# Eigenvalue counts beside a dense matmul stream: first loads on two queues, longer stated times, last products in twos, the last three groups in steps

**Chip and metric.** One core of a Trainium2 chip (trn2). The metric is the device time of one execution, in microseconds (us); lower is better. All numbers are medians of runs in the fast state unless a single profiled execution is named.

## The reference

Four residual layers, each `x = layernorm(x + layer(x))`, on x of 128 x 64 x 256 in fp32, with one 64 x 64 adjacency for all.

```python
# layer 0: three graph convolutions with adj*adj, widths 256 -> 512 -> 1024 -> 256
# layer 1: spectral: eigenvectors U of the normalised Laplacian, U (relu(U^T x W1 + b1) W2 + b2)
_, U = jnp.linalg.eigh(L_norm)
agg = jnp.einsum('mn,bnd->bmd', U.T, features)
# layer 2: two graph convolutions, then LSTMs over windows of 1, 2, 3 and 4 nodes
# layer 3: masked attention over the 64 nodes with shared h = x W + b
attention = jax.nn.softmax(scores, axis=2)
return jnp.einsum('bnm,bmd->bnd', attention, h) + b
```

## The kernel before

The rows of x are 64 tiles of 128 x 256. The kernel runs in two stages. In the first, layer 0 goes through 32 groups of two tiles, two groups in flight, and beside it runs the eigenvalue stream: the 64 x 64 matrix is made tridiagonal, the eigenvalues are bracketed by six passes of counting signs (a chain of small VectorE instructions and no matmul at all), then a recurrence gives the eigenvectors. In the second stage 16 groups of four tiles go through layers 1 to 3, three in flight.

TensorE's order is fixed while the program is built. Each stream is a generator; it yields the stated time at which its next matmul may come. A virtual clock `now` advances with each matmul:

```python
def mm(out, lhsT, rhs, start=True, stop=True):
    PE.matmul(out, lhsT, rhs, start=start, stop=stop)
    now[0] += 2 * max(0.0009 * rhs.free_size(), 0.112)
...
with tc.manual_schedule(engines={mybir.EngineType.PE}):      # TensorE, and no other engine
    while todo or going or eig:
        ...
        streams = ([eig] if eig else []) + going
        able = [x for x in streams if x[0] <= now[0] + 0.05]
        pick = able[0]          # or the earliest, and now moves on to it
```

The argument turns on the `with` line: the fixed order holds for TensorE only. Where the instructions of the other engines stand in their queues is decided by the framework.

The counts (`after(n)` adds 0.21 us per instruction to the stream's stated time):

```python
for k in range(1, N):
    V.reciprocal(r, Q[:, k - 1, :])
    V.scalar_tensor_tensor(Q[:, k, :], r, es[:, 0, k:k + 1], Q[:, k, :], op0=ALU.mult, op1=ALU.add)
    if k % 2:
        yield after(5)
```

The end of a layer 0 group; L626 is the addition, and the pool `psa` has five PSUM tiles:

```python
        S.copy(s3, p)
        yield now[0] + 1.5
        p = tl(psa, [P, 2, D], "ps")
        mm(p, sqT2, s3)
        V.tensor_add(xs, p, xs)                 # L626
        rows_norm(tc, small, xs, half)
```

The end of layer 3 (L911) and the choice among the last three groups:

```python
            for j in range(2):
                mm(p[:, j, :], eT[:, (t + j) * P:(t + j + 1) * P], hn[:, t + j, :])
                V.scalar_tensor_tensor(xs[:, t + j, :], p[:, j, :], sm[...], xs[:, t + j, :], ...)   # L911
...
    pick = able[0] if todo else min(able, key=lambda x: x[1])     # x[1]: turns taken so far
```

Of the kernel before, what the change touches and what calls it, by code (L numbers as in the profile page):

```python
# [39 lines left out]
def eigen(tc, stack, a, cst, u2, ut2, now):  # L40
# [8 lines left out]
    nc = tc.nc  # L49
# [10 lines left out]
    def ps(shape, tag):  # L60
        uid[0] += 1
        return pp.tile(shape, F32, tag=tag, name=f"{tag}_{uid[0]}")
# [6 lines left out]
    def after(n, turns=0):  # L69

        clock[0] += 0.21 * n + 0.6 * turns
        return clock[0] + 0.3
# [8 lines left out]
        V.scalar_tensor_tensor(junk, x, 1.0, y, op0=ALU.mult, op1=ALU.mult, accum_out=out)  # L81


    aT = ps([N, N], "pa")
    PE.transpose(aT, a, C["eye"])
    s2 = sb([N, N], "s2")
# [47 lines left out]
    for i in range(N - 2):  # L134
        j = i + 1
# [135 lines left out]
    for _ in range(PASSES):  # L271
        V.tensor_scalar(h, h, 1.0 / (FAN + 1), None, op0=ALU.mult)
        x = sb([N, FAN], "bx")
        V.tensor_scalar(x, C["idx"][:, 1:FAN + 1], h, lo, op0=ALU.mult, op1=ALU.add)
        V.tensor_tensor(Q, di[:, 0, :].unsqueeze(2).to_broadcast([N, N, FAN]),
                        x.unsqueeze(1).to_broadcast([N, N, FAN]), ALU.subtract)
        for k in range(1, N):
            r = sb([N, FAN], "br")
            V.reciprocal(r, Q[:, k - 1, :])  # L279
            V.scalar_tensor_tensor(Q[:, k, :], r, es[:, 0, k:k + 1], Q[:, k, :], op0=ALU.mult, op1=ALU.add)  # L280
            if k % 2:
                yield after(5)
        V.scalar_tensor_tensor(M.rearrange("p j k -> p k j"), Q, 0.0, inb.unsqueeze(2).to_broadcast([N, N, FAN]),
                               op0=ALU.is_lt, op1=ALU.mult)
        cnt = sb([N, FAN], "bx")
        V.tensor_reduce(cnt, M, AX.X, ALU.add)
        V.scalar_tensor_tensor(sb([N, FAN], "br"), cnt, tgt, C["ones"][:, :FAN], op0=ALU.is_le, op1=ALU.mult,
                               accum_out=co_[6])
        V.tensor_scalar(lo, co_[6], h, lo, op0=ALU.mult, op1=ALU.add)
        yield after(20)  # L290
# [8 lines left out]
    for k in range(1, N):  # L299
        c = N - 1 - k  # L300
        t = sb([N, 2], "tw")
        V.reciprocal(t, D[:, :, c + 1])
        V.tensor_mul(t, t, es[:, :, k])  # L303
        V.tensor_add(D[:, :, c], dl[:, :, k], t)
        if k % 2:
            yield after(6)
    V.tensor_scalar(D, D, 1e15, -1e15, op0=ALU.min, op1=ALU.max)
    V.tensor_add(t0, D[:, 0, ::-1], D[:, 1, :])
    V.tensor_sub(t0, t0, dl[:, 0, :])
# [20 lines left out]
    V.tensor_sub(zh, zd, oh)  # L330
    V.tensor_add(zh, zh, zu[:, ::-1])
    rowdot(nrm, zh, zh)
    yield after(24)
    pz = ps([N, N], "pa")
    PE.transpose(pz, zh, C["eye"])
    Z = cp.tile([N, N], F32, name="Z")
# [42 lines left out]
    rowdot(s1, zh, v1)  # L379
    rowdot(s1s, zh, v1s)  # L380
    rowdot(s2e, zh, v2)
    after(34)


    V.reciprocal(co_[6], nrm)
# [25 lines left out]
    V.tensor_mul(co_[12], co_[12], rn)  # L411


    yield after(16)
    pu = ps([N, N], "pa")
    mm(pu, Z, QT)
    UT = cp.tile([N, N], F32, name="UT")
    V.tensor_scalar(UT, pu, co_[12], None, op0=ALU.mult)
    yield after(1)
    pt = ps([N, N], "pb")  # L420
    PE.transpose(pt, UT, C["eye"])
    U = cp.tile([N, N], F32, name="U")
    V.tensor_copy(U, pt)
    V.memset(u2, 0.0)
    V.memset(ut2, 0.0)
    yield after(4, 1)
    for out, lhsT in ((u2, UT), (ut2, U)):
        p2 = ps([2 * N, N], "pa")
        for h in range(2):
# [7 lines left out]
D = 256  # L437
EPS = 1e-5
WAYS = 3


def rows_norm(tc, pool, x, half):
# [17 lines left out]
def kernel(  # L460
# [25 lines left out]
    nc = tc.nc  # L486
    V, S, PE = nc.vector, nc.scalar, nc.tensor
    NT = ROWS // P
    x_t = x.rearrange("b n f -> (b n) f").rearrange("(t p) f -> p t f", p=P)
# [22 lines left out]
    X = keep.tile([P, NT, D], F32, name="X")  # L512
# [2 lines left out]
    adst = keep.tile([P, N], F32, name="adst")  # L515
    a64 = ea.tile([N, N], F32, name="a64")
    eig_c = ea.tile([P, len(CONSTS), N], F32, name="eig_c")
    nc.sync.dma_start(a64, adj)
    for h in range(2):
        hs = slice(h * N, (h + 1) * N)  # L520
        nc.sync.dma_start(ad2[hs, hs], adj)
    nc.sync.dma_start(X[:, 0:2, :], x_t[:, 0:2, :])
    aw1 = load(wa, "aw1", a_w1, "(k p) f -> p k f", [P, 2, 512], p=P)
    nc.sync.dma_start(eig_c, consts)
    aw2 = wa.tile([P, 4, 1024], F32, name="aw2")
    for h in range(2):
        cols = slice(h * 512, (h + 1) * 512)
# [47 lines left out]
# [3 lines that stand above are left out]
# [53 lines left out]
    todo = [layer0(g) for g in range(NT // 2)]  # L631
    eig = [0.0, eigen(tc, phase_a, a64, eig_c, u2, ut2, now)]
    going = []
    with tc.manual_schedule(engines={mybir.EngineType.PE}):
        while todo or going or eig:
# [3 lines left out]
            able = [x for x in streams if x[0] <= now[0] + 0.05]  # L639
            if able:  # L640
                pick = able[0]
            else:
                pick = min(streams, key=lambda x: x[0])
# [32 lines left out]


    now[0] = 0.0
    MOVE, MIXED, LIN, CONV, NORM, SOFT = 1.2, 1.2, 1.5, 1.8, 4.5, 4.5
    CELL = {256: 2.6, 168: 2.2, 128: 1.9}  # L680

    def turn(out, in_):
# [12 lines left out]
    def as3(t, a):  # L695
        return t.rearrange("p (a b) -> p a b", a=a)
# [153 lines left out]
    def layer3(xs, g, ready):  # L850
        xT = as3(work(), 2)
        ps = [ps4() for _ in range(2)]
        for t in range(4):
            if t % 2 == 0:
                yield ready[t // 2]
            for k in range(2):
                turn(ps[k][:, t * P:(t + 1) * P], xs[:, t, k * P:(k + 1) * P])
        V.tensor_copy(xT[:, 0, :], ps[0])
        S.copy(xT[:, 1, :], ps[1])
        nc.gpsimd.tensor_tensor(xs, xs, wide["d_b"].unsqueeze(1).to_broadcast([P, 4, D]), ALU.add)  # L860
        yield now[0] + MOVE
        hT = as3(work(), 2)
        for c in range(2):
            p = ps4()
            run(p, [(dw[:, k, c * P:(c + 1) * P], xT[:, k, :]) for k in range(2)])
            S.activation(hT[:, c, :], p, AF.Identity, bias=dbl[:, c, :])
            yield now[0]
        yield now[0] + MOVE
        p = ps4((P, 4, N))
        for t in range(4):  # L870
            for h in range(2):
                cols = slice(t * P + h * N, t * P + (h + 1) * N)
                for k in range(2):
                    PE.matmul(p[h * N:(h + 1) * N, t, :], hT[:, k, cols], hT[:, k, cols], start=k == 0, stop=k == 1)  # L874
        now[0] += 1.5
        sc = as3(work2(), 8)
        s, z = sc[:, 0:4, :], sc[:, 4:8, :]
        V.tensor_mul(s, p, adst.unsqueeze(1).to_broadcast([P, 4, N]))
        V.tensor_scalar(z, s, 0.0, -1e16, op0=ALU.is_equal, op1=ALU.mult)
        V.tensor_add(s, s, z)  # L880
        mx = small.tile([P, 4], F32, name="mx")
        V.tensor_reduce(mx, s, AX.X, ALU.max)
        V.tensor_sub(s, s, mx.unsqueeze(2).to_broadcast([P, 4, N]))
        e = att[g % WAYS]
        for h in range(2):
            hs = slice(h * N, (h + 1) * N)
            S.activation(e[hs, :, hs], s[hs, :, :], AF.Exp)  # L887
        yield now[0]
        ready = now[0] + SOFT
        hn = as3(work(), 4)  # L890
        for t in range(0, 4, 2):
            p = ps4((P, 2, D))
            for j in range(2):
                for c in range(2):
                    turn(p[:, j, c * P:(c + 1) * P], hT[:, c, (t + j) * P:(t + j + 1) * P])
            S.copy(hn[:, t:t + 2, :], p)
        yield ready
        sm = small.tile([P, 4], F32, name="sm")
        p = ps4()
        for t in range(4):  # L900
            turn(p[:, t * P:(t + 1) * P], e[:, t, :])
        eT = work2()
        S.copy(eT, p)
        V.tensor_reduce(sm, e, AX.X, ALU.add)
        V.reciprocal(sm, sm)
        yield now[0] + MOVE
        for t in range(0, 4, 2):
            p = ps4((P, 2, D))
            for j in range(2):
                mm(p[:, j, :], eT[:, (t + j) * P:(t + j + 1) * P], hn[:, t + j, :])  # L910
                V.scalar_tensor_tensor(xs[:, t + j, :], p[:, j, :], sm[:, t + j:t + j + 1], xs[:, t + j, :],  # L911
                                       op0=ALU.mult, op1=ALU.add)
            rows_norm(tc, small, xs[:, t:t + 2, :], half)
            nc.sync.dma_start(out_t[:, 4 * g + t:4 * g + t + 2, :], xs[:, t:t + 2, :])
            yield now[0]

    def group(g):
        xs = X[:, 4 * g:4 * g + 4, :]
        ready = yield from layer1(xs)
        ready = yield from layer2(xs, ready)  # L920
        yield from layer3(xs, g, ready)



    todo = [group(g) for g in range(NT // 4)]
    going = []
    with tc.manual_schedule(engines={mybir.EngineType.PE}):
        while todo or going:
            while todo and len(going) < WAYS:
                going.append([0.0, 0, todo.pop(0)])  # L930
            able = [x for x in going if x[0] <= now[0] + 0.05]
            if not able:
                pick = min(going, key=lambda x: x[0])
                now[0] = pick[0]
            else:
                pick = able[0] if todo else min(able, key=lambda x: x[1])
            try:
                pick[0] = next(pick[2])
                pick[1] += 1
            except StopIteration:  # L940
                going.remove(pick)
# [42 lines left out]
```

## Time and profile before

| | before |
|---|---|
| time, median of the first three runs | 2721.07 us |
| TensorE busy in the profiled execution (2721.1 us) | 2593.5 us |
| TensorE idle, 0 to 68 us (start) | 14.8 us |
| TensorE idle, 408 to 748 us (counts to eigenvectors) | 31 us |
| TensorE idle, last slice of 68 us | 29 us |

The shares, slices and waits are shown in the prediction. There each digit of a slice row is a busy share in tenths, and PEclk is TensorE's granted clock, the share of full speed that it was allowed to run at (so 0.50 is half clock). The word *turn* is used twice: for the step that a stream gets from the scheduler, and for a transposition on TensorE (the function `turn`), as in "the norm's turn". A *cell* is an LSTM step. Two places of the timeline are worth a look of their own. Its columns are start, length, engine, line, operation, names, shapes, number of instructions and, in brackets, the engine's idle time before the row and what ended it. First TensorE in the count phase:

```profile
442.41 1.02 PE L576 MATMUL ps<-s,sqT 128*128 128x512 f32 x2
443.27 1.05 PE L576 MATMUL ps<-sqT,X 128*128 128x128 f32 x8
444.16 1.06 PE L576 MATMUL ps<-sqT,h 128*128 128x128 f32 x8
449.35 1.01 PE L576 MATMUL ps<-sqT,h 128*128 128x128 f32 x3 [4.13 <-DVE X L626]
```

And VectorE's (DVE) addition in the same stretch:

```profile
448.62 0.68 DVE L626 TENSOR_TENSOR X<-ps,X 128x512 f32<-128x512 f32 x1
```

The last product of a group (`ps<-s,sqT`) is done at 443.4, VectorE reads it at 448.62, 5.2 us later. In between TensorE has used the other four PSUM tiles, and it stands for 4.13 us until the fifth has been read. Then the end of layer 3 in the steady second stage:

```profile
1556.81 0.59 PE L576 MATMUL ps<-w,v 128*128 128x256 f32 x2
1558.43 1.13 PE L576 MATMUL ps<-w,v 128*128 128x256 f32 x4 [1.03 <-DVE X L911]
1560.14 0.70 PE L576 MATMUL ps<-w,v 128*128 128x256 f32 x2 [0.58 <-DVE X L911]
```

Each product waits until VectorE has read the one before it out of the same PSUM tile: 1.03 + 0.58 us per group.

### The profile page before, as it was taken

To read this page: it belongs to the slowest core of one execution; us is meant where nothing else is said; L and a number is where in the kernel's file an instruction comes from. 1 tells how busy PE (TensorE), PEld (TensorE's weight loads), DVE (VectorE), ACT (ScalarE), POOL (GpSimd) and SP (SyncE) were. 2 spreads that over 40 slices of the span, in tenths; PEclk is the share of its full clock that TensorE was granted. 3 is DMA by queue.
4 is the path that set the end of the run, shared out by engine and by line. 5 is a ranking of instruction groups with operands and counts; after the bars stand their busy time and mean duration, and the time that the engine had idled before them with its cause. 6 is when DMAs were issued, how large, how long until landed. Compare 5 with 4: busy or idle time off the path is not lost.

```text
span 2721.1 us, 39771 instructions
## 1 busy us (share of the span) xinstructions
PE 2593.5 (95%) x15384; PEld 2256.5 (83%) x15384; DVE 1334.8 (49%) x5277; ACT 1029.7 (38%) x2525; POOL 239.8 (9%) x336
## 2 busy tenths in 40 slices
PE   7999999999899989999999999999999999999995
PEld 6888877777688878898898898898898988978993
DVE  5777768888401033444444434445444444442335
ACT  2222222222122224544444544544444444445442
POOL 0000000000000020111101101101101101110012
PEclk9999999999899999999999999999999999999996
DMA  8000000000000010000000000000000000000000
GB/s 267 1 1 1 1 1 1 1 1 1 1 1 0 1 47 1 1 9 9 9 1 8 4 6 9 1 9 9 1 9 9 1 9 9 1 9 1 1 1 24
DMA packets 24398, 32.19 MB, mean 12 GB/s; under 512 B 2336, under 2 KB 21024, under 8 KB 24208
## 3 DMA queue, kind: packets, MB, share of 16 engines
q1 hardware_dynamic: 24032, 29.19, 3.2%
q8 instruction: 121, 1.98, 0.3%
q0 software_dynamic: 176, 0.46, 0.1%
q14 instruction: 69, 0.57, 0.1%
HBM read 21.25 MB, written 8.39 MB: 11 GB/s over the span
## 4 chain that ended last, share of the span: by engine, by line
PE 48%; DVE 4%; ACT 3%; POOL 2%; issue 1%; POOLq 0%; DVEq 0%; ACTq 0%
PE ps L576 47%; PE ps L683 1%; POOL ln_rs L453 1%; DVE X L455 1%; ACT gates L782 1%; DVE X L911 1%; ACT L887 1%; ACT L782 1%; DVE X L845 1%; PE ps L874 1%; DVE ln_st L450 1%; ACT att L887 0%; POOL ln_rs L452 0%; ACT gates L790 0%; DVE ln_mv L451 0%
## 5 line engine op out<-in xcount | busy, mean ns | idle before, releaser
L576 PE MATMUL ps<-w,wih 128*128 128x128 f32 (+2 forms) x4992 | 894.1, 319 | 3.5 <-DVE w L801 3.5
L576 PEld LDWEIGHTS ps<-w,wih 128*128 128x128 f32 x4992 | 763.8, 191 | 51.6 <-issue 10.1
L782 ACT ACTIVATE gates<-ps,cbi 128x128 f32<-128x128 f32 (+2 forms) x1248 | 500.4, 410 | 549.7 <-PE ps L576 542.1
L576 PE MATMUL ps<-hs,whh 128*128 128x128 f32 (+2 forms) x3072 | 537.5, 303 | 0.0
L576 PEld LDWEIGHTS ps<-hs,whh 128*128 128x128 f32 x3072 | 454.8, 191 | 24.9 <-issue 10.5
L576 PE MATMUL ps<-m,aw 128*128 128x256 f32 x2048 | 456.4, 381 | 2.1 <-DVE tw L303 2.1
L576 PEld LDWEIGHTS ps<-m,aw 128*128 128x128 f32 x2048 | 386.2, 190 | 64.2 <-issue 11.4
L584 ACT ACTIVATE h<-ps 128x256 f32<-128x256 f32 (+1 forms) x320 | 136.5, 426 | 445.3 <-PE ps L576 445.3
L576 PE MATMUL ps<-aw,h 128*128 128x256 f32 x1024 | 228.9, 380 | 0.0
L576 PEld LDWEIGHTS ps<-aw,h 128*128 128x128 f32 x1024 | 193.2, 190 | 36.7 <-issue 12.2
L787 DVE TENSOR_TENSOR gates<-gates 128x256 f32<-128x256 f32 (+2 forms) x256 | 92.6, 362 | 221.8 <-ACT gates L782 221.4
L452 POOL TENSOR_SCALAR ln_rs<-ln_mv 128x2 f32<-128x2 f32 x128 | 29.6, 231 | 1447.6 <-DVE ln_mv L451 1245.6
L455 DVE TENSOR_SCALAR X<-X,ln_mv,ln_rs 128x256 f32<-128x256 f32 x256 | 100.9, 433 | 107.2 <-POOL ln_rs L453 107.1
L790 ACT ACTIVATE gates<-c 128x128 f32<-128x128 f32 (+2 forms) x288 | 98.1, 341 | 96.1 <-DVE c L789 84.7
L801 DVE TENSOR_TENSOR w<-gates 128x256 f32<-128x256 f32 (+2 forms) x160 | 61.7, 395 | 147.7 <-PE ps L576 109.2
L626 DVE TENSOR_TENSOR X<-ps,X 128x512 f32<-128x512 f32 x32 | 21.8, 681 | 225.7 <-PE ps L576 225.7
L576 PE MATMUL ps<-aw,m 128*128 128x512 f32 x256 | 128.7, 628 | 0.0
L786 DVE TENSOR_TENSOR c<-c,gates 128x128 f32<-128x128 f32 (+2 forms) x192 | 63.8, 332 | 129.6 <-ACT gates L782 127.3
L792 DVE TENSOR_TENSOR hs<-gates 128x128 f32<-128x128 f32 (+2 forms) x192 | 62.9, 328 | 105.0 <-ACT gates L790 74.6
L837 POOL COPY w<-w 128x512 f32<-128x512 f32 x32 | 35.6, 1119 | 816.0 <-DVE w L801 594.3
L450 DVE BATCH_NORM_STATS2 ln_st<-X 128x6 f32<-128x256 f32 x256 | 99.5, 409 | 1.3
L279 DVE RECIPROCAL br<-Q 64x16 f32<-64x16 f32 x378 | 92.3, 244 | 12.2
(324 smaller groups left out, 2658.8 us busy)
## 6 DMA issues: line engine op xcount, KB each, us to landing
X<-in_x_dram SPq DMA_DIRECT2D x32, 256.0 KB, 6.2
out_dram<-X SPq DMA_DIRECT2D x32, 256.0 KB, 2.1
wih<-in_c_ih_dram SPq DMA_DIRECT2D x4, 1024.0 KB, 8.3
aw<-in_a_w_dram SPq DMA_DIRECT2D x3, 1024.0 KB, 11.3
whh<-in_c_hh_dram SPq DMA_DIRECT2D x3, 1024.0 KB, 5.5
aw<-in_a_w_dram SPq DMA_DIRECT2D x1, 512.0 KB, 6.7
cw<-in_c_w_dram SPq DMA_DIRECT2D x2, 256.0 KB, 4.0
bw<-in_b_w_dram SPq DMA_DIRECT2D x2, 128.0 KB, 4.2
```

What stands on the lines that cost most here:

```text
L279: V.reciprocal(r, Q[:, k - 1, :])
L450: nc.vector.bn_stats(st[:, t, :], x[:, t, :])
L455: nc.vector.tensor_scalar(x[:, t, :], x[:, t, :], mv[:, t, 0:1], rs[:, t:t + 1], op0=ALU.subtract, op1=ALU.mult)
L576: PE.matmul(out, lhsT, rhs, start=start, stop=stop)
L584: S.activation(dst, src, AF.Relu)
L782: S.activation(gate[q][:, h, :], pp, AF.Tanh if q == "g" else AF.Sigmoid, bias=bias[:, j:j + 1])
L786: V.tensor_mul(c[:, h, :], c[:, h, :], gate["f"][:, h, :])
L787: V.tensor_mul(to, gate["i"][:, h, :], gate["g"][:, h, :])
L790: S.activation(gate["i"][:, h, :], c[:, h, :] if p > 1 else to, AF.Tanh)
L792: V.tensor_mul(new[:, h, :], gate["o"][:, h, :], gate["i"][:, h, :])
L801: V.tensor_mul(hT[:, h, slice(first + p - 1, first + nw * p, p), :], gate["o"][:, h, :].rearrange("p (w b) -> p w b", b=8), gate["i"][:, h ...
L837: nc.gpsimd.tensor_copy(as3(hb[:, k, :], 8), hT[:, k, :, :].rearrange("p n b -> p b n"))
```

## The change

Five parts: the small first loads go out on ScalarE's queue beside SyncE's, and the eigenvalue stream starts at 4.0; the eigenvalue stream states longer times, so that TensorE should not wait for it; NORM and SOFT, the stated times of a norm and a softmax, grow; both products of a pair in layer 3 come before both reads; of the last three groups, the older ones lead by five turns.

```diff
+    yield 4.0
     aT = ps([N, N], "pa")
 ...
-                yield after(5)          # pair of count steps
+                yield after(6)
 ...
-            yield after(6)              # pair of recurrence steps
+            yield after(9)
 ...                                     # and 24->40, 34->44, 16->24, 1->3, (4, 1)->(8, 1)
-    nc.sync.dma_start(a64, adj)
 ...                                     # ad2, as before
-    nc.sync.dma_start(X[:, 0:2, :], x_t[:, 0:2, :])
+    for t in range(2):
+        nc.scalar.dma_start(X[:, t, :], x_t[:, t, :])
 ...                                     # aw1, as before
-    nc.sync.dma_start(eig_c, consts)
+    nc.scalar.dma_start(a64, adj)
+    nc.scalar.dma_start(eig_c, consts)
 ...
-    MOVE, MIXED, LIN, CONV, NORM, SOFT = 1.2, 1.2, 1.5, 1.8, 4.5, 4.5
+    MOVE, MIXED, LIN, CONV, NORM, SOFT = 1.2, 1.2, 1.5, 1.8, 5.2, 4.8
 ...
                 mm(p[:, j, :], eT[:, (t + j) * P:(t + j + 1) * P], hn[:, t + j, :])
+            for j in range(2):
                 V.scalar_tensor_tensor(xs[:, t + j, :], p[:, j, :], sm[...], xs[:, t + j, :],
 ...
+LEAD = 5
-                going.append([0.0, 0, todo.pop(0)])
+                going.append([0.0, 0, todo.pop(0), NT // 4 - len(todo)])
-                pick = able[0] if todo else min(able, key=lambda x: x[1])
+                pick = able[0] if todo else min(able, key=lambda x: x[1] + LEAD * x[3])
```

More of the change, by code (lines that the diff above doesn't have):

```diff
@@ L332, in eigen @@
     rowdot(nrm, zh, zh)
-    yield after(24)
+    yield after(40)
     pz = ps([N, N], "pa")
@@ L381, in eigen @@
     rowdot(s2e, zh, v2)
-    after(34)
+    after(44)
     V.reciprocal(co_[6], nrm)
@@ L411, in eigen @@
     V.tensor_mul(co_[12], co_[12], rn)
-    yield after(16)
+    yield after(24)
     pu = ps([N, N], "pa")
@@ L418, in eigen @@
     V.tensor_scalar(UT, pu, co_[12], None, op0=ALU.mult)
-    yield after(1)
+    yield after(3)
     pt = ps([N, N], "pb")
@@ L425, in eigen @@
     V.memset(ut2, 0.0)
-    yield after(4, 1)
+    yield after(8, 1)
     for out, lhsT in ((u2, UT), (ut2, U)):
```

## The prediction

> **What bounds the kernel now.** I began with the page: busy shares, then the 40 slices.
>
> ```profile
> PE 2593.5 (95%) x15384; PEld 2256.5 (83%) x15384; DVE 1334.8 (49%) x5277; ACT 1029.7 (38%) x2525; POOL 239.8 (9%) x336
> PE   7999999999899989999999999999999999999995
> DVE  5777768888401033444444434445444444442335
> PEclk9999999999899999999999999999999999999996
> ```
>
> TensorE is the bound nearly everywhere. Its order is fixed at build time by a virtual clock: each stream states when its next matmul may come, and the oldest (or the eigenvalue stream, always first) that is due gets the turn. So only TensorE's idle time, 2721.1 - 2593.5 = 128 us, and time at a low clock can be won. The table by stage (68 us each) says where it lies: 14.8 us in the first slice; 4.1, 4.1, 5.7, 5.8 and 11.5 in the slices from 408 to 748, where VectorE is 87% busy with the eigenvalue counts; 7.7 at the change to layers 1 to 3; about 2.7 a slice in their steady state; 29 in the last slice. The waits of TensorE give the causes, first of the whole run and then of 1020 to 2440 us:
>
> ```profile
> PE ps L576 <- DVE X L911: 26.8, 32, 1.8
> PE ps L683 <- DVE X L455: 23.4, 17, 4.0
> PE ps L576 <- DVE X L626: 17.6, 4, 5.7
> PE pa L85 <- DMA eig_c<-in_consts_dram: 11.0, 1, 11.0
> PE pa L335 <- DVE w L331: 11.0, 1, 11.0
> ...
> PE ps L576 <- DVE X L911: 20.1, 26, 1.0
> PE ps L683 <- DVE X L455: 10.9, 11, 1.0
> ```
>
> The columns are total us, times, longest. L626 and L331 are the count phase, L911 the last products of layer 3, L455 the norms, L85 the start. The table of short windows shows the second loss, the clock (its column PEclk follows the engines):
>
> ```profile
> 449.30:454.30 5.00, 4.95 (x12) 3.22 (x13) 4.06 (x19) 0.75 (x2) 0.93 (x2) 0.50 0.00 0
> 454.30:459.30 5.00, 5.00 (x24) 4.26 (x23) 4.36 (x19) 1.36 (x3) 0.00 (x0) 1.00 0.00 0
> 2646.60:2721.10 74.50, 41.95 (x230) 25.93 (x229) 41.27 (x117) 14.73 (x27) 23.48 (x32) 0.70 0.07 22
> ```
>
> After the 4.1 us wait at 449 TensorE ran 5 us at half clock: 12 matmuls where the next window has 24. In the last 74.5 us the clock averages 0.70.
>
> **What the Trainium skill says.** "TensorE: Matmul & The Clock Gate", section What's actually happening: the array's clock is halved after an idle window of about 3.4 us and restored after a busy one. The trace agrees (the two windows above), so a long wait costs more than its length. "PSUM — Partial Sum Buffer", section PSUM bank collisions: different engines must be kept apart by bank, not by address. The two 128x256 halves of a layer 3 pair fill one 2 KiB bank, so the second product must wait for VectorE's read of the first if it comes after it; the trace has that wait 32 times. "Perfetto Trace Analysis", Optimization Strategy: a bubble that repeats can mean too few PSUM buffers; at L626 it is so, layer 0 has five and TensorE stops at the one that L626 has not yet read, four times. "DMA: Bandwidth & Descriptors", Issuing engines are not separate DMA queues: a second issuer saves issue time only. The trace before has one big issuer; its packets already move 385 to 410 GB/s from 8 us on, so I expect no more bandwidth.
>
> **The change, part by part.**
>
> 1. Counts, after(5) to after(6) and others. A pair of count steps is stated at 5 x 0.21 = 1.05 us, a pass as 32 x 1.05 + 20 x 0.21 = 37.8. Stated time is not real time: a layer 0 group states 29.5 us, but has 130 matmul instructions, and the undisturbed slices from 748 on do 318 in 68 us, so 27.8 us: a factor 0.94. VectorE thus gets 35.6 us for a pass, but its reciprocals (L279) start a new pass every 42.6 us (405.1 to 618.0 in five). It falls 7 us behind per pass, and layer 0's addition L626 in the same queue starts 5 to 7 us late at 449, 511, 574 and 636, exactly the four waits. With 6: 32 x 1.26 + 4.2 = 44.5 stated, 42.0 real against 42.6, so nearly balanced; I leave 3 us for short remaining waits. The recurrence, 32 x 9 x 0.21 = 60.5 stated, 57 real, against 38 on VectorE (658.8 to 696.7), now has room to catch up, and after(40) gives 7.9 us for a chain of 4.5: the 11.0 at L335 and 2.1 at L303 go. Half clock: about 20 us were busy at it after these waits (5 after 449, 3.4 after 512, 5.7 after 575, 5.7 after 701), half of that, some 10 us, comes back. Sum 17.6 + 2.1 + 11.0 + 10 - 3 = **38 us**. The stream ends about 69 stated us later, near 750 of a layer 0 that ends near 940, so its later end costs nothing.
>
> 2. First loads. The first real matmul starts at 13.25 instead of perhaps 6.3 (the adjacency lands near 4.2, plus the 2.0 us that the trace shows from L568 to it). But in TensorE's order group 1's X tiles come next; they wait behind 2 MB of weights and landed at 17.1. They are issued 1.9 us earlier, so I estimate 15.2. Also L85 now stands between two halves of group 0, only 2 us of matmuls ahead of the product that needs its chain, and that chain took 4.0 us (11.03 to 15.06). So most of the 7 us at the start is turned into two other waits. **0.7 us** (0 to 2).
>
> 3. Last products in twos. Both products precede both reads, so the wait inside each pair goes: 1.03 + 0.58 = 1.61 per group. For 13 groups outside the tail the view has 20.1 us. **20 us.**
>
> 4. NORM 4.5 to 5.2, SOFT 4.5 to 4.8. In the steady state (period 105.1 us) 20 instructions, 5 gate units of 0.92 stated us, stand between the turns back and the turn of the first normed pair; 4.5 - 0.44 = 4.06 needs 5 units (4.61), 5.2 - 0.44 = 4.76 needs 6. So the turns come one unit, 0.86 real us, later, and the 0.99 us at the second pair shrinks to about 0.1: 11 x 0.86 = **9.5 us**. But that shifts the softmax too: the recurrent products of the two-step cell then follow their first step more closely, while ScalarE has its two table loads of 1.28 us and the exponentials beside it. I put a new wait of 0.8 us per group there: **-10 us**. Two half-clock windows (2086 and 2424, 3.4 us each) probably go: **+3 us**.
>
> 5. The last three groups in steps. Before, the one with fewest steps went first, so all three left the cells together at 2647 and went through the same latencies together: 74.5 us for 230 matmul instructions that need about 28 us at full clock. With LEAD = 5 the groups stay 5 and 10 steps apart; a four-step cell's step is 8 turns and 7.1 us, so group 14 is some 9 us of matmuls ahead of group 16, and its latencies lie beside those. I read what a lone group needs from its stages in the trace (copy back 2.2, turns, two norms of 3.5, products, softmax 2.2 + 2.2, output 2) as about 39 us, and add 13 to 15 for sharing. So some 54 instead of 74.5: **20 us**, the least certain term (8 to 30).
>
> Sum: 38 + 0.7 + 20 + 9.5 - 10 + 3 + 20 = 81 us; 2721.1 - 81 = **2640 us**.
>
> **Rivals.** (a) The count phase is VectorE's own rate and longer statements only move the stall. For it: VectorE is 87% busy there. Against: the TensorE order has 250 us of layer 0 without any eigenvalue work after 748 to put in between. If true, part 1 gives 10 us: 2668. (b) The new order in layers 1 to 3 makes TensorE wait for the cells (hs, L792) at every group, 2 us or more: for it, the ScalarE queue around the exponentials; against it, no wait on hs at all in the trace before. Then parts 3 and 4 give 5 us instead of 19.5: 2655. (c) The steps at the end leave the last group alone with its chain at half clock, and part 5 gives nothing: 2660; for it, five steps are only 4.5 us. (d) The start is really 7 us shorter, if the X tiles land much sooner: 2634; the 2 MB ahead speak against it.
>
> **Range and chances.** (b) and (c) each cost 15 to 20, seldom both with (a); on the other side the tail may give 10 more. Eight in ten: 2620 to 2665. The 2% line is 2721.07 x 0.98 = 2666.6; even with the tail at nothing and -5 elsewhere I am under it. Faster 0.91, same 0.08, slower 0.01.
>
> **What would show it.** Right: no waits on L626 above 2 us, none on L331, granted clock 1.00 in every slice from 408 to 952; TensorE's waits on L911 outside the tail near zero; the wait on L455 in the steady period near 0.1; a period near 103.4 us; the end phase 15 to 25 us shorter with idle TensorE below 20 us in it; the matmul after L85 and one on group 1's X waiting longer than before. Wrong: waits on L626 still in the count phase, waits on hs (L792) or w (L801) once per period, a tail as long as before, or a start that is 3 us or more shorter. Should the phases win what I say but the total not, the gain has gone into a new wait of the steady period.

## The result

| | before | after |
|---|---|---|
| median | 2722.86 us (4 runs) | 2688.89 us (4 runs) |
| ratio after to before | | 0.9876, 95% interval 0.9859 to 0.9893 |
| profiled execution | 2721.1 us | 2687.0 us |

A ratio is the mean time of one kernel's fast runs over that of the other's of the same rounds, so not quite the ratio of the medians quoted. The change is 1.2% faster: 34 us instead of the 81 predicted, outside the range, and short of the 2% that the prediction put at 0.91. The page after, the same lines as in the prediction:

```profile
PE 2585.3 (96%) x15384; PEld 2259.5 (84%) x15384; DVE 1345.3 (50%) x5277; ACT 1031.5 (38%) x2526; POOL 240.5 (9%) x336
PE   7999999999999999999999999999999999999995
DVE  4777768888510123335445445444444444453345
PEclk9999999999999999999999999999999999999997
```

VectorE still shows the plateau of 8 in the count phase, and now it ends in 5 and 1: the eigenvalue stream ends at 789 us instead of 728, as intended. But its counts run at the old pace: a new pass starts every 42.9 us (407.1 to 621.5 in five), before every 42.6. TensorE's waits over the whole run (total us, times, longest):

```profile
PE ps L579 <- DVE X L629: 25.6, 7, 6.5
PE ps L579 <- DVE hs L795: 14.3, 10, 1.4
PE ps L579 <- DVE w L710: 11.0, 4, 4.1
PE ps L686 <- ACT att L890: 8.5, 2, 6.2
PE ps L571 <- DMA ad<-in_adj_dram: 7.1, 1, 7.1
PE ps L686 <- DVE X L457: 5.2, 3, 3.1
...
PE ps L579 <- DVE sqT L573: 4.2, 1, 4.2
PE pa L75 <- DVE dm L114: 2.1, 1, 2.1
```

Lines have moved by two to four: L629 is the addition that was L626, L915 the read that was L911, L457 the norm's end that was L455. The waits on L915 and L331's successor are gone. But the wait on the addition has *grown*, from 17.6 to 25.6 us, and the new wait on `hs`, the cell's state, is 14.3 us. It comes ten times, once in a period, as here:

```profile
1546.71 0.70 PE L579 MATMUL ps<-hs,whh 128*128 128x256 f32 x2 [1.43 <-DVE hs L795]
```

The same place of the count phase as before, TensorE:

```profile
444.48 1.02 PE L579 MATMUL ps<-s,sqT 128*128 128x512 f32 x2
...
451.39 2.08 PE L579 MATMUL ps<-sqT,h 128*128 128x128 f32 x8 [4.11 <-DVE X L629]
```

and VectorE's addition there:

```profile
450.66 0.68 DVE L629 TENSOR_TENSOR X<-ps,X 128x512 f32<-128x512 f32 x1
```

It is the same picture, 2.0 us later: 4.11 us instead of 4.13.

To see where the 34.1 us come from, I took events that both traces have and compared their distances:

| stretch, from event to event | before | after | gain |
|---|---|---|---|
| start to the first wait after the tridiagonal form | 388.67 | 390.73 | -2.1 |
| from there to the last wait on layer 0's copy (L622, after L625) | 593.83 | 588.73 | 5.1 |
| from there to the norm's turn of the second stage at 1135 | 152.51 | 155.93 | -3.4 |
| from there to the same turn of the last steady group | 1247.69 | 1221.57 | 26.1 |
| from there to the end | 338.4 | 330.0 | 8.4 |

The first, second and last rows were to give 0.7, 38 and 20 us; the third and fourth together 22.5. Of the fourth row's 26.1 us, 9.7 lie in its first three periods (300.26 us before, 290.59 after) and 16.4 in the nine steady ones. For the last row, the end from the end of the last group's copy back, before and after (length, then busy us and instructions of TensorE, its loads, VectorE, ScalarE and GpSimd, then granted clock, DMA share and GB/s):

```profile
2652.00:2721.10 69.10, 38.93 (x216) 23.54 (x214) 36.75 (x109) 14.24 (x25) 18.15 (x28) 0.70 0.07 23
2632.60:2687.00 54.40, 30.03 (x147) 18.30 (x147) 29.34 (x84) 10.71 (x19) 12.07 (x18) 0.66 0.09 30
```

### The profile page after: what moved, and what is told of

It reads as the page before. It is cut to its first block, busy times and chain, and to the rows that moved or that the text cites. A ratio compares the mean times of both kernels' runs of the same rounds, so it can differ in the third digit from the quotient of the medians.

```text
span 2687.0 us, 39840 instructions
## 1 busy us (share of the span) xinstructions
PE 2585.3 (96%) x15384; PEld 2259.5 (84%) x15384; DVE 1345.3 (50%) x5277; ACT 1031.5 (38%) x2526; POOL 240.5 (9%) x336
## 3 DMA queue, kind: packets, MB, share of 16 engines
q8 instruction: 121, 1.98, 0.3%
## 4 chain that ended last, share of the span: by engine, by line
PE 50%; DVE 4%; ACT 2%; POOL 1%; issue 1%; POOLq 0%; DVEq 0%; ACTq 0%
PE ps L579 48%; PE ps L686 1%; DVE X L457 1%; POOL ln_rs L455 1%; DVE ln_st L452 1%; DVE X L848 1%; ACT gates L785 1%; PE ps L877 1%; ACT L785 0%; ACT L890 0%; POOL ln_rs L454 0%; ACT att L890 0%; DVE ln_mv L453 0%; DVE X L915 0%; DVE hs L795 0%
## 5 line engine op out<-in xcount | busy, mean ns | idle before, releaser
L579 PE MATMUL ps<-hs,whh 128*128 128x128 f32 (+2 forms) x3072 | 540.6, 303 | 14.4 <-DVE hs L795 14.3
L579 PEld LDWEIGHTS ps<-m,aw 128*128 128x128 f32 x2048 | 386.9, 191 | 66.1 <-issue 10.1
L579 PEld LDWEIGHTS ps<-aw,h 128*128 128x128 f32 x1024 | 193.1, 190 | 36.7 <-issue 12.2
L457 DVE TENSOR_SCALAR X<-X,ln_mv,ln_rs 128x256 f32<-128x256 f32 x256 | 104.3, 448 | 108.9 <-POOL ln_rs L455 108.9
L804 DVE TENSOR_TENSOR w<-gates 128x256 f32<-128x256 f32 (+2 forms) x160 | 73.9, 467 | 126.5 <-PE ps L579 81.5
L629 DVE TENSOR_TENSOR X<-ps,X 128x512 f32<-128x512 f32 x32 | 21.6, 676 | 208.5 <-PE ps L579 208.5
L840 POOL COPY w<-w 128x512 f32<-128x512 f32 x32 | 35.6, 1112 | 791.1 <-DVE w L804 791.1
```

Source lines behind the costliest of these rows:

```text
L457: nc.vector.tensor_scalar(x[:, t, :], x[:, t, :], mv[:, t, 0:1], rs[:, t:t + 1], op0=ALU.subtract, op1=ALU.mult)
L804: V.tensor_mul(hT[:, h, slice(first + p - 1, first + nw * p, p), :], gate["o"][:, h, :].rearrange("p (w b) -> p w b", b=8), gate["i"][:, h ...
L840: nc.gpsimd.tensor_copy(as3(hb[:, k, :], 8), hT[:, k, :, :].rearrange("p n b -> p b n"))
```

## The experiments

Fourteen kernels ran, all correct, each beside runs of the kernel before on the same chip. The question was first the count phase, where 33 of the missing 47 us were lost.

**Theories.** *Pace* (the prediction's): the stated times pace VectorE, so 6 instead of 5 per pair gives it enough time. *Order*: the framework lays out VectorE's queue from its own estimate of durations; stated times set TensorE's order alone. (How the framework decides was not looked into; what the runs can show is only whether the stated times decide.) *Rate*: VectorE is too slow for counts beside layer 0 in whatever order.

The queues of the built programs can be read without a chip. How many of the 378 count steps stand on VectorE before the additions of layer 0 groups 13 to 20:

```text
before         26  66 123 164 211 252 309 349
after          26  66 123 163 210 252 307 347
e_counts       26  66 123 163 210 252 307 347
e_dve5         23  68 126 171 222 265 316 368
e_dve6         19  63 106 141 189 228 269 313
e_dvecount     19  63 106 141 189 228 269 313
e_dvecount7    17  55  88 126 159 189 230 259
```

The change moved at most two steps. That was the reason to form the order theory. The traces agree: counted there, the steps that had started before these additions are the same within one.

**The counts alone** (`e_counts`): the kernel before with the longer stated times of the eigenvalue stream.

```diff
-                yield after(5)
+                yield after(6)
 ... (and the other six statements)
```

> The kernel before with the longer stated times of the counts and the rest of the eigenvalue stream, and nothing else. Theory of the prediction (stated times pace VectorE): the waits of TensorE on the addition of layer 0 and the one on L331 go, 38 us faster, near 2684. Rival 1 (order theory: VectorE's order is laid out by the framework from its own estimate of durations, the stated times set TensorE's order alone): the addition still stands behind 66, 163, 252, 347 count steps, its four or five long waits stay (some 25 us together), only the 11.0 us before L335 goes: 3 to 8 us faster, near 2717. Rival 2 (rate theory: VectorE is too slow for the counts beside layer 0, whatever the order): the same as rival 1 here.

Measured: 2722.95 us, ratio 0.9992 (0.9984 to 1.0001); 25.6 us of waits on the addition. The pace theory falls: 38 us became about 2, with an interval that includes none; the order theory had left 3 to 8. A pass still takes 42.9 us. The 11.0 us at L335 are gone, but most of it is now paid at the addition: 25.6 us instead of 17.6, with one more long wait, 5.66 us at 704.

**VectorE in the fixed order too, stated 6 and 5** (`e_dve6`, `e_dve5`): the changed kernel with

```diff
-    with tc.manual_schedule(engines={mybir.EngineType.PE}):
+    with tc.manual_schedule(engines={mybir.EngineType.PE, mybir.EngineType.DVE}):
```

around the first stage; `e_dve5` also takes the pair of count steps back to `after(5)`.

> The changed kernel with VectorE in the fixed order of the first stage too, so that stated times (6 per pair) set its order as well. Order theory: before the additions of layer 0 stand fewer count steps (19, 63, 106, 141 instead of 26, 66, 123, 163), the additions start within 2 us of their product, TensorE waits for them under 5 us in all instead of 25.6, no half clock from 408 to 748: about 30 us faster than the changed kernel, near 2658. Rate theory: the waits stay as they are, near 2689.

> The same with the old statement of 5 per pair of count steps. Order theory, with the prediction's arithmetic (37.8 us stated, 35.6 real, 42.6 needed per pass): the queue falls 7 us behind per pass, waits on the addition of 20 us or more come back, near 2682 to 2690. If the fixed order alone were what helps, as near 2658 as with 6. Rate theory: 2689 for both.

Measured: 2698.26 us (0.9906) with 6, 2727.09 us (1.0012) with 5. Both are slower than the changed kernel; the number expected for 6 was missed by 40 us, the one for 5 by 37 or more. TensorE's waits over the whole run say why (total us, times, longest). `e_dve6`:

```profile
PE pc L75 <- DVE junk L152: 19.5, 11, 2.6
PE ps L579 <- DVE hs L795: 14.4, 10, 1.4
PE ps L579 <- DVE X L629: 11.4, 5, 4.4
```

And the same waits of TensorE in `e_dve5`:

```profile
PE ps L579 <- DVE X L629: 26.8, 9, 8.1
PE pc L75 <- DVE junk L152: 19.5, 11, 2.6
```

In the fixed order the wait on the addition does follow the stated time: 11.4 us with 6, 26.8 us with 5, and 29 us of total time between them, where all the longer statements together make 2 us in the framework's order. But the fixed order is bad for the tridiagonal part before the counts (L152, 19.5 us in 11 waits, against 0.8 us in two in the changed kernel), and that costs more than the 14.2 us won at the addition. The next run tests this reading.

**The fixed order in the counts only** (`e_dvecount`, `e_dvecount7`): a second region for VectorE is entered when the counts start and left after the recurrence; `e_dvecount7` also states more.

```diff
+            if steered[0] and not fixed:
+                fixed.append(tc.manual_schedule(engines={mybir.EngineType.DVE}))
+                fixed[0].__enter__()
+            elif fixed and not steered[0]:
+                fixed.pop().__exit__(None, None, None)
 ...                                   # e_dvecount7 only:
-                yield after(6)
+                yield after(7)
-        yield after(20)
+        yield after(28)
```

> The changed kernel with VectorE in the fixed order only from the counts to the end of the recurrence, so that the stated 6 per pair sets VectorE's order there and nowhere else. Order theory: the waits on the addition of layer 0 fall from 25.6 us to about 11 (what the run with the whole first stage fixed showed), the waits on L152 that that run got before 400 us are gone, and it is 15 to 22 us faster than the changed kernel: near 2670. If that run's slower time had another cause than the order of the part before the counts: still near 2698.

> The same with 7 instead of 6 per pair of count steps and 28 instead of 20 at the end of a pass: 53 us stated, 50 real for the 42.6 that VectorE needs. Order theory: no wait on the addition above 1 us, no half clock from 408 to 748, 30 us faster than the changed kernel: near 2658. Debt theory (VectorE's time is the bound of the count phase in any order): no better than with 6.

Measured: 2669.34 us (0.9791) and 2653.93 us (0.9735, interval 0.9721 to 0.9750). Both numbers of the order theory were met within 5 us. `e_dvecount` differs from the changed kernel in VectorE's order alone and is 19.5 us faster; its waits on the addition are 10.1 us, and two of the five slices from 408 to 748 still have a clock of 0.95. So 6 is too little even in the fixed order. In `e_dvecount7` the table by stage shows what the prediction had promised (busy us of TensorE, its loads, VectorE, ScalarE, GpSimd, then granted clock and DMA):

```profile
408.00:476.00 68.00, 68.00 (x324) 56.22 (x323) 52.96 (x205) 16.92 (x41) 1.85 (x4) 1.00 0.00 1
476.00:544.00 68.00, 68.00 (x322) 56.49 (x322) 53.07 (x201) 17.49 (x44) 2.77 (x6) 1.00 0.00 1
```

TensorE is busy all 68 us at full clock, 324 matmul instructions where the kernel before has 288, and from the first count to the last the additions start 0.04 us after their products. In the fixed order the pass does follow the statement: one starts every 43.9 us with 5 (`e_dve5`), 45.8 with 6 (`e_dvecount`) and 50.2 with 7 (409.0 to 659.9 in five), against 42.9 in the changed kernel. The rate theory falls: VectorE can do all the counts beside layer 0, if its queue spreads them over more of layer 0.

**Another reader for the PSUM tile** (`e_evac`): the changed kernel, with ScalarE copying the last product out of PSUM.

```diff
-        V.tensor_add(xs, p, xs)
+        s4 = pa.tile([P, 2, D], F32, tag="s4", name=f"s4_{g}", bufs=1)
+        S.copy(s4, p)
+        V.tensor_add(xs, s4, xs)
```

> The changed kernel with layer 0's last product copied out of PSUM by ScalarE into SBUF, and added by VectorE from there, so that its PSUM buffer is free without VectorE. If TensorE's waits in the count phase are waits for that buffer (order and rate theory both), they go, though the additions still come 5 to 8 us late: waits on the addition 0 instead of 25.6, no half clock from 408 to 748, about 30 to 35 us faster than the changed kernel, near 2655. If TensorE waits for VectorE in another way, nothing changes: 2689.

Measured: 2686.97 us (0.9864), 2 us better than the changed kernel instead of 30 to 35, and with overlapping intervals (0.9849 to 0.9879 against 0.9859 to 0.9893) no gain that is shown. The waits on the addition are gone, and two others have come. TensorE's from 400 to 760 us (total, times, longest):

```profile
PE ps L579 <- ACT h L587: 22.2, 1, 22.2
PE ps L579 <- ACT s L630: 6.0, 1, 6.0
```

And ScalarE's (ACT) from 600 to 760 us:

```profile
ACT co L340 <- DVE junk L81: 30.5, 1, 30.5
```

This is the most instructive miss. With nothing holding TensorE, the additions come later and later: 2.4, 5.9, 9.6, 13.0, 17.1, 20.7, 24.2, 27.8, 32.3 and 36.7 us behind their products, 3.4 to 4.5 us more with each, 3.8 on average. Then ScalarE reaches a square root of the eigenvalue stream (L340) in its queue, stands there for 30.5 us until VectorE has caught up, and TensorE stands behind ScalarE for 22.2. In this order VectorE's queue carries a debt of some 36 us, and freeing the tile did not lower it; the small waits at the addition were its instalments. What removed it in these runs was the other order with the counts spread further (`e_dvecount7`).

**The first loads alone** (`e_loads`), the kernel before with part 2 only:

> The kernel before with the first loads on two queues and the 4.0 at the start of the eigenvalue stream alone. Prediction: 0.7 us faster (0 to 2). Rival, read from the changed kernel's trace: its first product of the eigenvalue stream comes at 25.48 us instead of 23.42, because VectorE stands in order behind the constants (landed at 10.47 on the second queue) before it may copy the transposed adjacency, and because 2.07 us are waited for the chain behind L85: 2 us slower, near 2728 where before is 2726.

Measured: 2729.27 us, ratio 1.0012 (1.0005 to 1.0018), so about 3 us slower. The rival holds, with some spread: 5 of the 20 runs lie between 2723.9 and 2724.9, no slower than before, and 15 between 2728.4 and 2730.8. TensorE's waits at the start, 14.3 us in three before, are now 17.8 in four:

```profile
PE ps L570 <- DMA ad<-in_adj_dram: 8.1, 1, 8.1
PE ps L578 <- DVE sqT L572: 5.5, 1, 5.5
PE pa L75 <- DVE dm L114: 2.1, 1, 2.1
PE ps L578 <- DMA X<-in_x_dram: 2.1, 1, 2.1
```

and VectorE's row in the changed kernel tells where the second comes from:

```profile
10.57 0.22 DVE L81 SCALAR_TENSOR_TENSOR junk<-a,eig_c 64x64 f32<-64x64 f32 x1 [9.32 <-DMA eig_c<-in_consts_dram]
...
11.12 0.28 DVE L572 COPY adT<-ps 128x128 f32<-128x128 f32 x1
11.43 0.29 DVE L573 TENSOR_TENSOR sqT<-adT 128x128 f32<-128x128 f32 x1
```

TensorE had the transposed adjacency ready at 7.6, but VectorE stood at an instruction that needs the constants, which landed at 10.47 on the second queue, and it took its instructions in order. When the constants land differs between executions: 10.47 in the changed kernel, 12.76 in `e_loads` with the same loads. The Trainium skill's page "DMA: Bandwidth & Descriptors", Issuing engines are not separate DMA queues, says that transfers of all issuers run on the same DMA engines and interleave. The traces agree as far as they go: the first tiles of X landed by 5.51 instead of 7.77, but the second half of the adjacency, issued at 1.83 instead of 1.98 and now behind the first weights, landed at 6.98 instead of 5.54.

**Twos and norms alone** (`e_twos_norm`), the kernel before with parts 3 and 4:

> The kernel before with the last products in twos and NORM 5.2, SOFT 4.8 alone. Prediction: the waits on L911 outside the tail go (20 us), the one on L455 in the steady period shrinks from 0.99 to about 0.1, a new wait on the cell's state of 1.4 us per group comes (as in the changed kernel), the period is 103.4 us: 20 to 28 us faster than before, near 2697. If the steady period's gain in the changed kernel came from another part: less than 10 us.

Measured: 2702.57 us, ratio 0.9913: 23.5 us (2726.06 to 2702.57). The waits from 1140 to 2380 are those of the changed kernel to the line: 14.3 us on `hs` in ten waits of 1.43, and no other above 0.8. The steady gain is these two parts' (a period of 103.44 us). So is the loss at the change of stages: the wait of 4.09 us at 1013.8 on the copy L707 stands in this trace too, and not in that of the steps alone.

**The steps alone** (`e_lead`), the kernel before with part 5:

> The kernel before with the last three groups in steps (LEAD 5) alone. The prediction gave it 20 us (8 to 30); the changed kernel's last stage, from the last common turn of the 13th steady group to the end, was only 8.4 us shorter than before. If the steps alone do that: 6 to 10 us faster, near 2714. If the other parts (twos, NORM) had eaten a larger gain: 15 us or more.

Measured: 2718.20 us, ratio 0.9975 (0.9965 to 0.9986), 6.8 us, in the range expected of the steps alone; nothing ate a larger gain.

**How far apart** (`b_lead5`, `b_lead15`, `b_lead40`): `e_dvecount7` with the first loads of the kernel before again, and LEAD 5, 15 or 40.

> The run with 7 per pair and VectorE's order fixed in the counts, with the first loads of the kernel before again. If the two queues cost 2 us or more, 2 to 4 us faster than with them (2653.9): near 2651. If they don't: 2654.

> The same with LEAD 15 instead of 5. Theory A (the last group's chain took 55 us instead of the estimated 39 because the two groups only 5 and 10 steps ahead still share VectorE, GpSimd and ScalarE with it): further apart it is shorter, 4 to 10 us faster than LEAD 5. Theory B (a lone group at half clock is the floor, and a larger lead only takes other work from beside it): the same or slower, within 3 us of LEAD 5.

> The same with LEAD 40, so that the last three run almost one after the other. Theory A: no slower than LEAD 15. Theory B: slower than LEAD 5 by 5 us or more, because the last group then has TensorE alone for part of its cells, where each step waits for its own state.

Measured: 2652.55 (0.9732), 2651.27 (0.9727), 2654.28 us (0.9736). Taking the loads back is worth 1.4 us (2653.93 to 2652.55, on another chip, with overlapping intervals), less than expected and not clear of noise. The three leads differ by less than their intervals. Yet the traces differ much. From the end of the last group's copy back (L849 here) to the end of the program the chain takes 54.5 us with LEAD 5, 40.2 with 15 and 35.1 with 40; but that copy ends at 2596.6, 2609.1 and 2618.0. What the last group's chain gains by being alone, its cells lose by coming later. Theory A's mechanism is seen and its gain is not. Theory B fits LEAD 15, but not LEAD 40, which it put 5 us or more above LEAD 5 and which is 1.7 us above.

**The wait on the cell's state** (`b_cell`, `b_soft`): `b_lead15` with the stated time of a 256 wide cell step 4.1 instead of 2.6, or with SOFT 4.5 again.

> LEAD 15, VectorE's order fixed in the counts, first loads of before, and the stated time of a 256 wide cell step 4.1 instead of 2.6. If the new wait of 1.43 us per group on the cell's state (hs) is a cell step stated too short beside the softmax's table loads: the ten waits go, 10 to 14 us faster than 2651.3, near 2639. If something else holds TensorE at that place (the softmax's exponentials for the oldest group): the wait moves to another line and the time stays within 4 us of 2651.

> The same base with SOFT 4.5 instead of 4.8 and CELL 2.6 as it was. If the longer SOFT alone (not NORM) brought the softmax and the recurrent products so close that hs is waited for: the 1.43 us per group go, near 2637 to 2641. If NORM 5.2 shifted it: the waits stay, near 2651.

Measured: 2677.44 us (0.9825) and 2656.41 us (0.9745). `b_cell` misses both of its numbers. In `b_soft` 17.1 us of waits on `hs` are still there (the time is 5 us above the one expected for that): SOFT alone is not the cause. NORM, which shifts all that follows by one gate unit, and the products in twos are left; neither was tried alone, so the cause stays open. In `b_cell` the waits on `hs` fall to 2.3 us, and the order that takes their place is worse:

```profile
PE ps L695 <- DVE X L461: 21.6, 24, 1.3
...
PE ps L582 <- ACT v L744: 7.4, 11, 0.7
```

The period rises from 103.45 us to 104.7: about 1 us of it is more waiting. In 8 of 11 periods a stretch of 3.4 us at half clock follows as well, which costs 1.7 us more (106.4). One stated time moved the whole order, and removing the wait that it aimed at cost more than the wait.

**The best version.** `b_lead15`, 2651.27 us, beats both kernels: 0.9727 of before (0.9711 to 0.9744), 38 us below the change. `b_lead5` is as good within the interval.

## Why the prediction was wrong

- **Part 1, the counts: wrong.** The step that failed is "VectorE thus gets 35.6 us for a pass" and with it "With 6: 32 x 1.26 + 4.2 = 44.5 stated, 42.0 real against 42.6, so nearly balanced". The stated times did not pace VectorE: its queue was laid out by the framework, the longer statements moved it by at most two steps, and a pass took 42.9 us after as 42.6 before. What was right is that there is a debt, but it is smaller than said. "It falls 7 us behind per pass": in `e_evac` it grows by 34.3 us over nine additions, in which TensorE's own order moves on by 247.4 us, so by about 5 us in the 35.6 us of a pass. And "nearly balanced" was too hopeful even where statements do pace VectorE: with 6 in the fixed order 10.1 us of waits are left where 3 were put (`e_dvecount`); 7 removes them. In the trace the part gave 5.1 us instead of 38, alone about 2. I had read the `manual_schedule` line and knew its engines, and did not ask who orders the rest. Rival (a) was nearer in size, 10 us, but its cause, VectorE's own rate, is refuted by `e_dvecount7`.
- **Part 2, the loads: sign wrong.** The X tiles landed at 15.76 (15.2 estimated), and the wait for the chain behind L85 was 2.07 as foretold. The step that failed is "instead of perhaps 6.3": the first real matmul came at 11.78, because the adjacency landed at 6.98 and not near 4.2, and because TensorE then waited 4.22 us for VectorE, which stood in order behind the constants. The first stretch lost 2.1 us instead of winning 0.7.
- **Part 3: right.** All 32 waits on L911 are gone.
- **Part 4: mechanism right, the sum partly by luck.** The second turn waits 0.12 instead of 0.99, and the period is 103.45 where 103.4 was foretold. But the new wait on the cell's state is 1.43 us per group where 0.8 was put. Per steady group the foretold terms of parts 3 and 4 make 1.61 + 0.86 - 0.8 = 1.67, and the measured gain is 105.08 - 103.45 = 1.63; with 1.43 in the place of 0.8 they make 1.04. TensorE's idle time in the period fell by no more than 1.15 us (2.71 to 1.56); the other 0.48 is busy time (102.37 to 101.89) that the prediction did not have. Of the two half-clock stretches that should go, the one at 2086 went and the other is still there (3.4 us from 2383). Nor were two larger amounts foreseen: 3.4 us lost at the change of stages, and nearly half of the 9.7 us won in the first three periods (three times 1.67 are 5.0), where among others waits of 2.28 and 1.21 us on L801 went. So 22.7 us of 22.5 for both parts is not a confirmation of every term. Rival (b) was half right: TensorE does wait for the cells in every steady group, but 1.43 us and not 2 or more, and the two parts together still won.
- **Part 5, the steps: mechanism right, size wrong.** "So some 54 instead of 74.5": the 74.5 us count from the end of the last cells (2646.6). From there the changed kernel takes 60.0 us (2627.0 to 2687.0), so this end won 14, not 20. From the end of the copy back it is 54.4 us (2632.6 to 2687.0) against 69.1 before, 14.7 us. The other mis-sized term is the start of that chain: the copy comes 284.5 us after that of the last steady group, not 278.2, as layer 3 of the two leading groups now lies before the last cells (the three leads agree: the larger the lead, the later the copy). 14.7 - 6.3 = 8.4 us.
- **The tests that the prediction named.** "no waits on L626 above 2 us" and "granted clock 1.00 in every slice from 408 to 952" failed and pointed at part 1 at once; "a period near 103.4 us", "TensorE's waits on L911 outside the tail near zero", none on L331 and about 0.1 at L455 held. "Idle TensorE below 20 us" in the end phase did not: it was 26.5 us in those 60.0. Rivals (c), no gain from the steps, and (d), a start 7 us shorter, did not come. Three readings were loose, without weight in the sum: VectorE is 87% busy from 408 to 680, but 48% in the slice to 748; the 385 to 410 GB/s last until 14 us and are 344 to 363 after it; and the eigenvalue stream ends at 789, not near 750.

Alone, the parts (`e_counts`, `e_loads`, `e_twos_norm`, `e_lead`) change the ratio by -0.08, +0.12, -0.87 and -0.25%: -1.08% in all against -1.24% together. The remaining 0.16% lies within the sum of their intervals and was not pursued.

## What to carry to other kernels

Before a stated time, a priority or a buffer is changed to remove a wait, ask which engine's queue is late and who decides its order; here the order of VectorE was not the one that the statements steer, and counting in the built program how many instructions stand ahead of the late one would have shown it without a chip. In `e_evac` a late queue was a debt: another reader of the buffer only moved the day of payment, and on the later day two engines stood. When work is moved out of an end phase, add what it pushes back before counting the shorter end as gain.

## What the Trainium skill lacked or had wrong

- "Perfetto Trace Analysis", Optimization Strategy, takes a repeating bubble as a sign that PSUM or SBUF may be short. Here that was not enough: with the tile freed by ScalarE the bubbles went (25.6 us) and came back as one wait of 22.2 us and one of 6.0, because VectorE's queue was 36.7 us late. The section does say to look for what the engine waits for and to make it start sooner; it doesn't say that a reader can be late by its place in its own queue, and that buffers then only defer the wait.
- No page that I read has a case of what it costs when the head of a queue waits and ready work stands behind it: VectorE stood 9.32 us at an instruction that needed the constants, the last 2.9 of them (7.6 to 10.47) with the transposed adjacency ready for it, and ScalarE 30.5 us at one square root.
- "TensorE: Matmul & The Clock Gate", section What's actually happening, ties half clock to an idle window of about 3.4 us, which runs freely. That fits the waits of 4.1 to 5.7 us here, and also one of 3.70 us (637 us, before) that left the clock at 1.00, since it need not fill a window. What the section doesn't give is how much of a window must be idle: a wait of 3.02 us (577.9 us, changed kernel) was followed by half clock, and so were, in `b_cell`, three waits of 0.68, 0.48 and 1.34 us within 5 us.
